# Block 1's norms on GpSimd, with the context rows loaded a job ahead

## The chip, the cores and the metric

The kernel runs on one core of a Trainium2 chip. A core has a matrix engine (PE, with its weight loads shown as PEld), VectorE (DVE), ScalarE (ACT), GpSimd (POOL) and SyncE (SP), which work side by side and wait for one another by semaphores. Data are in on-chip memory (SBUF), in the eight accumulator banks of PSUM, or in DRAM, from and to which DMA moves them. Each engine runs its own instructions in a fixed order, so an instruction that waits holds up all those behind it on its engine. A DMA is issued by one engine's queue and then runs by itself.

The metric is the device time of one execution, in microseconds, taken as the median of the runs; lower is better.

## The reference

The input is x, 16 batches × 256 rows × 512 channels in float32, a context of the same shape, and a padding mask. Two blocks run over x. The first (block 0) is a cross-attention block with a GELU MLP. The second (block 1) is the one that the change touches. Cut to its steps, with 16 heads of 32 channels:

```python
def layer(x, context):
    m0 = (any of x[b, s, :] != 0)          # rows in use, as 0 or 1
    x = layer_norm(x + mha(x, x, Wq1, Wk1, Wv1, m0, causal=True), ln1_g, ln1_b)
    m1 = (any of x[b, s, :] != 0)
    x = layer_norm(x + mha(x, context, Wq2, Wk2, Wv2, m1, causal=False), ln2_g, ln2_b)
    h = relu(x @ fc1_w.T + fc1_b) * m0
    x = layer_norm(x + (h @ fc2_w.T + fc2_b) * m0, ln3_g, ln3_b)
    return x

def _mha(x, kv, Wq, Wk, Wv, mask, causal):
    Q, K, V = x @ Wq, kv @ Wk, kv @ Wv     # per head, times the mask
    energy = Q @ K.T
    lengths = number of columns with energy[.., 0, :] != 0
    energy = -inf where column >= lengths (and where column > row, if causal)
    return (softmax(energy / sqrt(32)) @ V) * mask
```

Where the reference spells steps out with einsum, they stand here in words. The kernel masks the context's rows before the products with Wk2 and Wv2, which is the same as masking K and V. A layer norm subtracts the row's mean, multiplies by the inverse of its standard deviation, multiplies by a gain per channel and adds an offset per channel.

## The kernel before

Rows are handled in eight groups of two batches, which is 512 rows or four tiles of 128 rows × 512 channels. Block 1 has sixteen jobs: eight groups of self-attention (n = 0 to 7), then eight of cross-attention (n = 8 to 15). Its MLP over the eight groups comes behind them. A job has eight units (i, c), two batches by four sets of four heads, so 32 heads.

The main stream of job n − 1 (scores, softmax, values) is woven together with `feed(n)`, which makes what job n needs: q, k and v by matrix products, the transposes of its inputs, and the lengths of the rows in use. The order of PE's instructions is thereby written out by hand. The orders of DVE, ACT, POOL and SP come from a scheduler, which plays the program through on a timeline with its own estimates of durations and puts each instruction where it would be ready. Changing durations, buffers or engines of some instructions therefore moves others too.

What the change and the steps of the prediction touch:

- `ln_stats` (L244 to L248): the statistics of a tile (BN) and the variance plus epsilon on DVE, and the power −0.5 on POOL (L248). `layer_norm` adds two operations of DVE in which a row's mean or scale and a table of gains or offsets enter (L257, L258).
- `Mha.norm` (L1436 to L1443): when all channels of a batch's two tiles are through, their norms are queued in `att.later`. For a self job `nonzero` (L1369, DVE) then tests the finished rows, which gives the mask m1; the rows are stored to DRAM by SP (L1442). Later jobs load them again (`rows_of`, L1492) into one of three x tiles.
- `finish` (L1464 to L1473): z is scaled from PSUM to SBUF by DVE (L1466) and added to the x tile by POOL (L1473).
- `context_rows` (L1549 to L1552) loads one 128 × 512 tile of the context by SP; the tag `t512` with three places holds it, and also `junk` of the test and the MLP's `relu` and `y`. `context` (L1554 to L1562) multiplies it by m1 on POOL (L1559), transposes it on PE (L283, into `ps_t`), and asks for the tile three further on.
- `project_t` (L264) makes q and k; `split` (L131, L135, L136) takes them from PSUM as a high and a low half; `keep` (L384) stores them as `d` in DRAM, and `build` (L395, L399, L404) loads them again as `stack`, the shape that the scores need.
- `lengths` (L1397 to L1417) makes the row bias from the first token's energies: PE (`ps_e`, L1397), DVE (`lbias`, L1405 to L1413), and a small DMA to `dbias` (L1417). `first_token` (L1378, L1380, split at L139 and L140) prepares the first token's q.
- The scores (L414, `ps_s`, two PSUM banks), their row minimum in cross jobs (L425, L429, `mn`), the exponential on ACT (L439, `e`), the transposes of it (L455, `ps_pt`; taken out by DVE L459 or ACT L461, `pt`), and the reciprocal sums `rr` (L1451, L1452).
- The weights of the next kind of job are loaded in steps of the same queue, `att.later`, and split by POOL (L195, L198).
- `norm_table` (L1536 to L1546) loads a table of gains and offsets, broadcast to 128 partitions: ln1 in job 0, ln2 at the end of job 8's feed, and ln3 before the MLP. Two tables have places at a time (tag `lnt`).
- In the MLP, `up` makes relu (L1650) and its halves, and `down` makes `y` on ACT (L1656), adds it on POOL (L1657), and ends with a layer norm and the store to the output (L1661).

SP's DMAs use eight semaphores in a ring, so that a DMA is not issued before the one eight places earlier has landed.

Of the kernel before, what the change touches and what calls it, by code (L numbers as in the profile page):

```python
# [42 lines left out]
def kernel(ctx: ExitStack, tc: tile.TileContext, a, out):  # L43
# [1377 lines left out]
    def block1(mlp0):  # L1421
        tables, more = {}, {}

        class Mha(Job):
# [111 lines left out]
        def norm_table(name, n):  # L1536
            t = tables[name] = pool.tile([P, 2, C], F32, tag="lnt", name=name)
            rows = a[name].rearrange("o (r c) -> o r c", c=C)
            nc.sync.dma_start(
                out=t.rearrange("p r c -> p (r c)"),  # L1540
                in_=bcast(rows[:, :2].rearrange("o r c -> o (r c)"), 2 * C),
            )
            if n == 3:
# [5 lines left out]
        def context_rows(n, t):  # L1549
            if n < len(jobs) and jobs[n].cross and (n, t) not in cxs and t < G:  # L1550
                cx = cxs[n, t] = pool.tile([P, C], F32, tag="t512", name="cx", bufs=3)
                nc.sync.dma_start(out=cx, in_=of("ctx", jobs[n].g)[:, t, :])  # L1552

        def context(n, t):  # L1554
            job = jobs[n]
            if t == 0:
                job.c_t = inputs("c_t")
            cx = cxs[n, t]
            nc.gpsimd.tensor_scalar(cx, cx, job.m[:, t : t + 1], None, ALU.mult)  # L1559
# [23 lines left out]
        def feed(n):  # L1583
# [5 lines left out]
            for c in range(KC):  # L1589
# [34 lines left out]
            for t in range(3 if n + 1 > NG else 2):  # L1624
# [4 lines left out]
            if n == NG:  # L1629
                norm_table("ln2", 2)  # L1630
# [14 lines left out]
        def up(g, c):  # L1645
# [3 lines left out]
            r = pool.tile([P, N], F32, tag="t512", name="relu", bufs=3)  # L1649
# [3 lines left out]
        def down(g, t):  # L1653
            x = xs[g][:, t, :]
            y = pool.tile([P, C], F32, tag="t512", name="y", bufs=3)
# [4 lines left out]
            layer_norm(pool, x, tables["ln3"][:, 0, :], tables["ln3"][:, 1, :])  # L1660
# [84 lines left out]
```

## Time and profile before

| | |
|---|---|
| runs | 2740.61, 2741.23, 2743.34 us |
| median | 2741.23 us |
| profiled execution | 2734.54 us |
| its span, first to last instruction | 2732.8 us |
| mean granted PE clock | 0.993 |
| PE busy | 2655.3 us, 97% |
| DVE busy | 2053.2 us, 75% |
| ACT busy | 1816.8 us, 66% |
| POOL busy | 604.5 us, 22% |
| block 1 in the trace | from about 1370 us to the end |
| a steady self job | 66.3 us |
| a steady cross job | 74.7 us |

The profiled execution is one run; what lies in it between the span and its time is 1.74 us. Busy time of an engine counts its instructions' durations. A line of waits names the engine and line that waited, the engine and line that it waited for, the total, the count and the longest. A line of a group names the line, the engine, the operation, its output and inputs with shape and type, the count, the busy time, and the mean of one in nanoseconds, then the idle time before it and what ended that. A stretch of the span is told as its bounds, its length, the busy time of PE, PEld, DVE, ACT and POOL with counts, PE's granted clock, the share of DMA time and its rate.

### The profile page before, as it was taken

To read this page: it belongs to the slowest core of one execution; us is meant where nothing else is said; L and a number is where in the kernel's file an instruction comes from. 1 tells how busy PE (TensorE), PEld (TensorE's weight loads), DVE (VectorE), ACT (ScalarE), POOL (GpSimd) and SP (SyncE) were. 2 spreads that over 40 slices of the span, in tenths; PEclk is the share of its full clock that TensorE was granted. 3 is DMA by queue.
4 is the path that set the end of the run, shared out by engine and by line. 5 is a ranking of instruction groups with operands and counts; after the bars stand their busy time and mean duration, and the time that the engine had idled before them with its cause. 6 is when DMAs were issued, how large, how long until landed. Compare 5 with 4: busy or idle time off the path is not lost.

```text
span 2732.8 us, 56709 instructions
## 1 busy us (share of the span) xinstructions
PE 2655.3 (97%) x19030; PEld 2245.1 (82%) x19030; DVE 2053.2 (75%) x5963; ACT 1816.8 (66%) x5278; POOL 604.5 (22%) x676
## 2 busy tenths in 40 slices
PE   8999999999899999999989999999999999999998
PEld 6777777777899999999978877887777777777787
DVE  7776667757846569999957777777778777777887
ACT  4877777778555555444547888877777777777522
POOL 2222212114301101111221111115212222113334
PEclk9999999999999999999999999999999999999999
DMA  6666556556323344443475656667666665565321
GB/s 231 189 194 182 171 173 190 186 166 174 112 112 136 124 163 171 166 169 140 155 232 174 192 192 195 196 199 213 183 198 191 190 194 183 183 189 161 104 90 51
DMA packets 287808, 465.40 MB, mean 170 GB/s; under 512 B 36256, under 2 KB 188320, under 8 KB 279328
## 3 DMA queue, kind: packets, MB, share of 16 engines
q1 hardware_dynamic: 287520, 461.78, 52.5%
q8 instruction: 153, 2.51, 0.4%
q14 instruction: 135, 1.11, 0.1%
HBM read 284.97 MB, written 176.69 MB: 169 GB/s over the span
## 4 chain that ended last, share of the span: by engine, by line
PE 80%; DVE 11%; DMA 3%; issue 3%; ACT 2%; POOL 1%; SPq 0%; POOLq 0%; DVEq 0%; ACTq 0%
PE ps_p L264 20%; PE ps_v L264 15%; PE down L1142 10%; PE ps_pt L455 9%; PE ps_s L414 6%; PE ps_z L474 6%; PE up_sc L1026 5%; PE up_pt L1026 3%; PE up_mm L1026 3%; PE ps_t L283 2%; ACT e L439 1%; DVE st L244 1%; DVE e L429 1%; DVE c_t L145 1%; PE ps_z L1464 1%
## 5 line engine op out<-in xcount | busy, mean ns | idle before, releaser
L439 ACT ACTIVATE e<-e,mn 128x256 f32<-128x256 f32 (+1 forms) x1024 | 487.5, 481 | 58.5 <-DVE mn L429 56.4
L461 ACT COPY pt<-ps_pt 128x512 f32<-128x512 f32 (+1 forms) x696 | 378.6, 547 | 175.8 <-PE ps_pt L455 163.8
L455 PE MATMUL ps_pt<-ident,e 128*128 128x128 f32 x2816 | 435.5, 273 | 14.5 <-DVE lbias L1406 7.9
L455 PEld LDWEIGHTS ps_pt<-ident,e 128*128 128x128 f32 x2816 | 336.1, 140 | 53.9 <-ACT pt L461 6.5
L414 PE MATMUL ps_s<-stack 97*128 97x256 f32 (+1 forms) x1536 | 331.6, 297 | 12.4 <-ACT e L439 5.6
L414 PEld LDWEIGHTS ps_s<-stack 97*128 97x128 f32 (+1 forms) x1536 | 268.6, 190 | 72.8 <-ACT e L439 13.2
L439 ACT ACTIVATE e<-ps_s,mn 128x256 f32<-128x256 f32 x512 | 241.4, 484 | 53.2 <-DVE mn L425 42.9
L1142 PE MATMUL down<-w_h,c_t 128*128 128x256 f32 x900 | 255.5, 285 | 5.4 <-DVE c_t L145 5.4
L1473 POOL TENSOR_TENSOR x<-x,zz 128x256 f32<-128x256 f32 x128 | 95.8, 748 | 724.6 <-DVE zz L1466 671.0
L1142 PE MATMUL down<-w_h,x_t 128*128 128x256 f32 x868 | 245.8, 283 | 0.7 <-ACT x_t L144 0.7
L1142 PE MATMUL down<-w_l,x_t 128*128 128x256 f32 x868 | 246.2, 284 | 0.0
L429 DVE CUSTOM_DVE_ANT_0 e<-mb,ps_s 128x256 f32<-128x256 bf16 x512 | 192.7, 415 | 70.6 <-PE ps_s L414 68.7
L248 POOL TENSOR_TENSOR rstd<-rstd,nhalf 128x1 f32<-128x1 f32 x192 | 141.0, 740 | 385.0 <-DVE rstd L247 384.3
L264 PE MATMUL ps_p<-x_t,q_h 128*128 128x512 f32 x640 | 215.3, 417 | 4.2 <-DVE qk L131 2.1
L425 DVE TENSOR_REDUCE mn<-ps_s 128x2 f32<-128x512 f32 x256 | 175.3, 685 | 49.2 <-PE ps_s L414 47.0
L429 DVE CUSTOM_DVE_ANT_0 e<-tri,ps_s 128x128 f32<-128x128 f32 (+1 forms) x512 | 160.2, 346 | 54.9 <-PE ps_s L414 52.9
L474 PE MATMUL ps_z<-pt,v 128*32 128x256 f32 (+1 forms) x3072 | 198.2, 368 | 2.0 <-DVE pt L459 1.9
L439 ACT ACTIVATION_READ_ACCUMULATOR e<-e,mn 128x1 f32 x1024 | 197.6, 193 | 0.0
L1142 PEld LDWEIGHTS down<-w_h,c_t 128*128 128x128 f32 x900 | 171.3, 191 | 7.3 <-DVE c_t L145 7.3
L1142 PEld LDWEIGHTS down<-w_h,x_t 128*128 128x128 f32 x868 | 166.5, 192 | 1.1 <-ACT x_t L144 0.9
L1142 PEld LDWEIGHTS down<-w_l,x_t 128*128 128x128 f32 x868 | 165.2, 190 | 0.0
L474 PEld LDWEIGHTS ps_z<-pt,v 128*32 128x32 f32 x3072 | 82.3, 109 | 98.4 <-issue 28.5
(256 smaller groups left out, 7232.0 us busy)
## 6 DMA issues: line engine op xcount, KB each, us to landing
stack<-d SPq DMA_DIRECT2D x1152, 128.0 KB
d<-qk SPq DMA_DIRECT2D x192, 512.0 KB
hid<-ho SPq DMA_DIRECT2D x32, 1024.0 KB
raw<-hid SPq DMA_DIRECT2D x32, 1024.0 KB
x<-xd SPq DMA_DIRECT2D x128, 256.0 KB
xd<-x SPq DMA_DIRECT2D x96, 256.0 KB
xin<-in_x_dram SPq DMA_DIRECT2D x32, 256.0 KB
xr<-in_x_dram SPq DMA_DIRECT2D x32, 256.0 KB
```

Source lines behind the costliest of these rows:

```text
L248: nc.gpsimd.tensor_tensor(out=rstd[:, 1:2], in0=rstd[:, 0:1], in1=nhalf, op=ALU.pow)
L264: nc.tensor.matmul(ps, w[p], x[q], start=(k == 0 and i == 0), stop=(k == kc - 1 and i == 2))
L414: nc.tensor.matmul(ps[:, t, :], u.st[: self.rows, 0, j, ts(t, P)], u.st[: self.rows, 1, j, :], start=True, stop=True,)
L425: nc.vector.tensor_reduce(mn, ps, AX.X, ALU.min)
L429: nc.vector.tensor_tensor_reduce(out=e[:, at], in0=bias[t], in1=ps[:, t, : job.width[t]], scale=-SC, scalar=BIG, op0=ALU.add, op1=ALU.min, ...
L439: nc.scalar.activation(e[:, at], ps[:, t, :] if bias is None else e[:, at], AF.Exp, bias=mn[:, t : t + 1], scale=-1.0, accum_out=u.rs[:, t ...
L455: nc.tensor.transpose(pp[:, ts(x, P)], e[:, at : at + P], ident)
L461: nc.scalar.copy(pt[:, :n], pp[:, :n])
L474: nc.tensor.matmul(z[ts(j, D), w[0] * P :], job.v[u.i * NT + mc][:, u.c * P + j * D : u.c * P + (j + 1) * D], u.pt[j][:, x0 * P : (x0 + le ...
L1026: nc.tensor.matmul(ps[:, mm, :], w[p][:, k, :], x[q][:, k, :], start=(first and mm == k == j == 0), stop=(k == 1 and j == 2), skip_group_c ...
L1142: nc.tensor.matmul(ps[:, t, :], x[p][:, mm, ts(t, P)], w[r][:, bo, :], start=(q == mm == t == j == 0), stop=(q == self.NS - 1 and mm == 1 ...
L1473: nc.gpsimd.tensor_tensor(out=xv, in0=xv, in1=zz, op=ALU.add)
```

## The change

The sixty norms of block 1's attention jobs other than the last cross group's four leave DVE for POOL after the statistics: one operation with mean and scale, one multiplication by the gain table, one addition of the offset table. The stores of these rows go by POOL's queue. The test of a self job's rows writes bfloat16 into a place of its own.

Context rows have four places of their own (tag `cx`). All four tiles of a job are asked for in the feed of the job before, `context` asks for none, and DVE masks them. The tables of norms share one place; ln2 is asked for in job 9's feed, behind the second q product, and ln3 is loaded as two tiles into context places. The MLP's `relu` and `y` take places of the tags `e` (five) and `pts` (six).

```diff
+    def layer_norm_pool(pool, x, gain, offset):
+        mean, rstd = ln_stats(pool, x)
+        nc.gpsimd.tensor_scalar(x, x, mean, rstd, ALU.subtract, ALU.mult)
+        nc.gpsimd.tensor_tensor(out=x, in0=x, in1=gain, op=ALU.mult)
+        nc.gpsimd.tensor_tensor(out=x, in0=x, in1=offset, op=ALU.add)
...
             def norm(self, t):
                 x, table = self.x[:, t, :], tables["ln2" if self.cross else "ln1"]
-                layer_norm(pool, x, table[:, 0, :], table[:, 1, :])
+                last = self.cross and self.g == NG - 1
+                norm = layer_norm if last else layer_norm_pool
+                norm(pool, x, table[:, 0, :], table[:, 1, :])
                 if not self.cross:
-                    junk = pool.tile([P, C], F32, tag="t512", name="junk", bufs=3)
+                    junk = pool.tile([P, C], BF16, tag="junk", name="junk", bufs=1)
                     nonzero(junk, x, m1[:, self.g, t : t + 1])
-                nc.sync.dma_start(
+                (nc.sync if last else nc.gpsimd).dma_start(
                     out=xd[3 if self.cross else 2][self.g][ts(t, P), :], in_=x
                 )
...
         def norm_table(name, n):
-            t = tables[name] = pool.tile([P, 2, C], F32, tag="lnt", name=name)
             rows = a[name].rearrange("o (r c) -> o r c", c=C)
...
-            if n == 3:
+            if n == 2:
+                t = tables[name] = pool.tile([P, 2, C], F32, tag="lnt", name=name, bufs=1)
...
+            else:
+                tables[name] = [pool.tile([P, C], F32, tag="cx", name=name, bufs=4) for r in range(2)]
+                for r, t in enumerate(tables[name]):
+                    nc.sync.dma_start(out=t, in_=bcast(rows[:, r], C))
...
-                cx = cxs[n, t] = pool.tile([P, C], F32, tag="t512", name="cx", bufs=3)
+                cx = cxs[n, t] = pool.tile([P, C], F32, tag="cx", name="cx", bufs=4)
...
-            nc.gpsimd.tensor_scalar(cx, cx, job.m[:, t : t + 1], None, ALU.mult)
-            cost = transposed(job.c_t, cx, t)
-            context_rows(n, t + 3)
-            return cost
+            nc.vector.tensor_scalar(cx, cx, job.m[:, t : t + 1], None, ALU.mult)
+            return transposed(job.c_t, cx, t)
...
+                if n == NG + 1 and c == 1:
+                    norm_table("ln2", 2)
                 if job.cross:
                     for t in FRONTS[c]:
-                        context_rows(n, t)
                         yield context(n, t)
...
-            for t in range(3 if n + 1 > NG else 2):
+            for t in range(G):
                 context_rows(n + 1, t)
...
-            if n == NG:
-                norm_table("ln2", 2)
...
-            r = pool.tile([P, N], F32, tag="t512", name="relu", bufs=3)
+            r = pool.tile([P, N], F32, tag="e", name="relu", bufs=5)
...
-            y = pool.tile([P, C], F32, tag="t512", name="y", bufs=3)
+            y = pool.tile([P, C], F32, tag="pts", name="y", bufs=6)
...
-            layer_norm(pool, x, tables["ln3"][:, 0, :], tables["ln3"][:, 1, :])
+            layer_norm(pool, x, *tables["ln3"])
```

By the scheduler's order PE's instructions stand as before. DVE has 120 operations fewer (60 each of L257 and L258) and 32 more (the masks). POOL has 32 operations fewer, 180 more, and 60 DMA issues. SP has 60 stores fewer. The loads of job 8's four context tiles, and their masks, are moved by it to job 0's time at the beginning of block 1, since their places are free from the start.

More of the change, by code (lines that the diff above doesn't have):

```diff
@@ L1536, in norm_table @@
         def norm_table(name, n):
-            t = tables[name] = pool.tile([P, 2, C], F32, tag="lnt", name=name)
             rows = a[name].rearrange("o (r c) -> o r c", c=C)
[L1539 to L1542, printed above, removed]
-            if n == 3:
+            if n == 2:
+                t = tables[name] = pool.tile([P, 2, C], F32, tag="lnt", name=name, bufs=1)
+                nc.sync.dma_start(
+                    out=t.rearrange("p r c -> p (r c)"),
+                    in_=bcast(rows[:, :2].rearrange("o r c -> o (r c)"), 2 * C),
+                )
+            else:
+                tables[name] = [pool.tile([P, C], F32, tag="cx", name=name, bufs=4) for r in range(2)]
+                for r, t in enumerate(tables[name]):
+                    nc.sync.dma_start(out=t, in_=bcast(rows[:, r], C))
                 t = tables["fc2_b"] = pool.tile([P, C], F32, name="fc2_b", bufs=1)
```

## Prediction

> **What bounds the kernel now.** I read the totals by engine, the chain that ended last, the stretches of block 1, then PE's waits there, then the groups of instructions that the change touches.
>
> ```profile
> span 2732.8 us, 56709 instructions
> PE 2655.3 (97%) x19030; PEld 2245.1 (82%) x19030; DVE 2053.2 (75%) x5963; ACT 1816.8 (66%) x5278; POOL 604.5 (22%) x676
> PE 80%; DVE 11%; DMA 3%; issue 3%; ACT 2%; POOL 1%; SPq 0%; POOLq 0%; DVEq 0%; ACTq 0%
> ```
>
> PE is busy for 97% of the span. No edit here takes a matmul away, so whatever is gained must come out of PE's idle time (and out of the clock lost behind it), and whatever is lost is new PE idle time. The stretches give it by stage (us, then PE, PEld, DVE, ACT, POOL busy with counts, then PE clock, DMA share, GB/s): all of block 1, a steady self job, the last self job with the change to cross jobs, the first cross job, a steady cross job, the MLP end, and two pieces of the change.
>
> ```profile
> 1370.00:2732.80 1362.80, 1317.88 (x9008) 1053.63 (x9008) 1036.90 (x3339) 938.71 (x3025) 326.76 (x345) 0.99 0.56 176
> ...
> 1562.60:1628.90 66.30, 65.42 (x482) 52.91 (x481) 50.62 (x237) 53.22 (x185) 9.59 (x12) 1.00 0.60 192
> 1827.80:1896.30 68.50, 64.70 (x460) 51.47 (x459) 49.93 (x226) 49.61 (x172) 28.53 (x30) 0.95 0.75 228
> 1896.30:1971.00 74.70, 69.70 (x499) 56.12 (x498) 55.72 (x227) 55.09 (x188) 23.00 (x24) 0.98 0.65 199
> 2120.30:2195.00 74.70, 73.31 (x531) 58.12 (x530) 58.50 (x145) 55.64 (x180) 14.91 (x16) 1.00 0.59 185
> 2570.00:2732.80 162.80, 154.15 (x706) 123.82 (x704) 130.25 (x249) 44.43 (x71) 64.11 (x57) 0.98 0.23 81
> ...
> 1876.00:1884.00 8.00, 4.83 (x33) 3.15 (x31) 4.47 (x19) 3.16 (x13) 6.85 (x8) 0.74 0.96 229
> 1908.00:1916.00 8.00, 5.64 (x35) 4.57 (x37) 6.42 (x26) 4.73 (x17) 5.34 (x5) 0.84 0.63 214
> ```
>
> A steady self job leaves 0.9 us of PE idle in 66.3, a cross job 1.4 in 74.7; DVE and POOL have room in both. What PE waited for in block 1 (total, times, longest):
>
> ```profile
> PE ps_pt L455 <- DVE lbias L1406: 7.9, 7, 3.2
> PE ps_e L1397 <- ACT qk L135: 5.2, 1, 5.2
> PE ps_s L414 <- DVE rr L1452: 3.0, 5, 0.6
> PE ps_t L283 <- POOL cx L1559: 3.0, 2, 2.4
> PE ps_p L264 <- DVE qk L131: 2.1, 1, 2.1
> ```
>
> Five of the seven lbias waits are about 0.87 us each, one in a steady cross job; the 3.2, the 2.4 and the 2.1 are the change to cross jobs (1877 to 1915 us). The five rr waits are 0.6 each, one per self job. All the PE gaps that I could list behind 1370 us add up to 36.5 us: the ceiling of any gain before clock.
>
> **The change part by part.** These are the groups that it moves (us busy, mean ns):
>
> ```profile
> L257 DVE SCALAR_TENSOR_TENSOR x<-x,mv,ln 128x512 f32<-128x512 f32 x96 | 77.1, 805 | 0.0
> L258 DVE SCALAR_TENSOR_TENSOR x<-x,rstd,ln 128x512 f32<-128x512 f32 x96 | 70.5, 741 | 6.7 <-POOL rstd L248 6.1
> L1559 POOL TENSOR_SCALAR cx<-cx,m 128x512 f32<-128x512 f32 x32 | 51.6, 1613 | 68.9 <-DMA cx<-in_ctx_dram 65.9 <-PE ps_p L264 1.3 <-DVE mn L429 1.0
> L1657 POOL TENSOR_TENSOR x<-x,y 128x512 f32<-128x512 f32 x32 | 44.1, 1407 | 46.5 <-ACT y L1656 46.5
> ```
>
> *Norms.* 60 of the 64 norms of block 1's jobs move (the last cross group and the MLP's 32 stay). DVE loses 60 × (0.805 + 0.741) = 92.8 us. POOL gains 60 × (1.61 + 2 × 1.41) = 266 us, priced by its mask row and its y-add row; for three operations of 2-input kind it would be 254, and with the subtract-and-multiply at the slowest mask seen (1.96) 287. Per job of four tiles DVE drops by 6.2 us, POOL rises by 17.7: a self job from 9.6 to 27 of 66, a cross job to 26 of 75 after its masks leave. POOL stays under 45%.
>
> *Masks.* 32 operations leave POOL (−51.6 us) and join DVE. DVE has no such row: 0.42 (the 128x512 cast, L139) from below, 0.68 (L1369) from above; I take 0.48, nearer the cast, so +15 us. DVE net: −6.2 a self job, −4.3 a cross job.
>
> *What this is worth on PE's path.* The 0.6 us (self) and 0.87 us (cross) gaps come just behind DVE's burst of statistics and norms, where DVE comes late to rr or lbias. Taking 3.1 us of norm operations out of each burst of two tiles should close most. Five self gaps × 0.6 gives 3.0 and five cross gaps × 0.87 gives 4.4, both taken whole. Bounds: 0 and 7.4.
>
> *The change to cross jobs.* The 2.36 us wait on a masked cx row goes, since job 8's four tiles are now loaded and masked at the beginning of block 1. The 2.11 on qk (DVE in its burst) I halve. The 3.17 on lbias has DVE itself waiting 1.42 us for a small DMA, and the ACT ahead of it 2.30 for DVE; I halve it too. Sum 2.4 + 1.05 + 1.6 = 5.0, bounds 2.4 and 7.6. Behind these gaps the granted clock fell to 0.74 and 0.84. With the 0.83 and 0.95 of the neighbouring 8 us, (1 − clock) × busy adds up to 3.8 us; I take half, 1.9.
>
> The Trainium skill, "TensorE: Matmul & The Clock Gate", Part 1, says that PE's clock halves after an idle window of about 3.4 us and comes back after as long a busy one. The 0.74 stands behind a gap of only 3.17 us here; by that rule no gap left would cost clock, all 3.8 us would come back, and the sum would be 1.9 us lower.
>
> *New wait: DVE on a context row.* In a steady cross job a mask no longer waits on POOL but in DVE's order, two running minima (L425) behind the last q split (L131). SP issues the store of that split first and the next job's rows straight behind (0.34 + 0.38 us by SP's rows). Rows land 3.80 us after issue (row at 2054.75) up to 5.93 (1984.20). A head takes 74.7/32 = 2.33 us, so DVE is there some 2.5 to 3.5 us after the split and waits 1 to 4 us (0.72 + 3.80 − 3.5 to 0.72 + 5.93 − 2.5) for a mask that nobody needs for a job. Behind it stand L425, L459 and the rr of the running heads. PE has two score banks, so about 1.9 us pass free; cost 0 to 2.2 us a job, I take 0.6 × 7 = +4.2 (a wait of 2.5, the middle; bounds 0 and +15), because three of the four masks stand further behind their load.
>
> *New wait: DVE on POOL.* The nonzero test (L1369) of a self job reads the finished norm. By the order it stands seven heads (14.5 us or more) behind the statistics; POOL's row of work for two tiles, two pow at 0.89, the residual add L1473 at 0.75 and 2 × 4.4, ends 11.3 us after them if POOL is not held. Slack 3 us: cost 0, bound +1 us × 8. The cover is gone if POOL's operations here run a quarter slower.
>
> *POOL's queue.* 60 stores go to POOL, 60 of SP's 64 leave L1442. No row has a store issued by POOL: by SP's rows 0.3 to 0.43 each; bound 0 to one mask (1.6). On POOL that is at most 6.4 us a job, in free time. Each job's x loads (L1492) wait until the stores of two jobs before have landed, now 8 us later; in the steady jobs 7 to 9 us remain before PE's transposes. SP is in order, and stack builds behind it (L395, L399, L404) have some 13 us. Cost 0, bound +1 us × 13.
>
> The Trainium skill, "SBUF — State Buffer", "SBUF: two separate sides", speaks against this: GpSimd and a DVE instruction with two SBUF inputs take one port pair exclusively, and descriptors for a GpSimd-issued DMA are starved meanwhile; it advises issuing from SP or ACT. No such store is in this trace. By the page's example (620 ns grown to 3100) each store would be 2.5 us later, a third of the slack above, so the sum would stay.
>
> *Sharing.* DVE operations that overlap POOL are longer here: the small tok cast (L139) 0.17 us alone, 0.49 on average beside POOL. Added over 1430 to 2570 us this is 5.8 us. POOL's 327 us becomes about 540, so DVE's excess grows by 3.8 us over 15 jobs; I put +0.5 on PE's path.
>
> *Start of block 1.* Job 8's 4 × 256 KB replace the ln3 load there, 512 KB ahead of the k store instead of 768 KB, 768 KB more behind. The 5.2 us wait on ACT qk (behind d<-qk, landing 7.75 us) may shrink by 1; later stores come later. Taken +1, bounds ±3.
>
> *MLP end.* relu and y change rings (five and six places), ln3 sits in two cx places. The same operations on the same engines; 0, bounds ±1.
>
> Sum: −3.0 − 4.4 − 5.0 − 1.9 + 4.2 + 0.5 + 1.0 = −8.6. The profiled execution took 2734.5 us, so 2725.9 in its terms. It lies 6.7 us below the median of the runs (2741.2), which gives 2732.6. A difference of 0.2% (5.5 us) is about what a measurement of this kernel can tell.
>
> **Rivals.**
>
> *A. DVE stands at a mask or a test, slower.* Place: the first mask of each steady cross job. If the row lands 7 us behind its issue (a d<-qk store took 7.75 at 1400), DVE waits some 4.5 us, PE loses 2.6 × 7 = 18, and gaps of that length pull the clock as at 1877 (1.2 us each), 8 more. The other terms of the sum give −12.8, so +13, about 2754. It decides from a wait of 3.7 us: 1.8 over PE's free 1.9, × 7 = 12.8. For it: POOL waited for cx rows 23 times, up to 5.8 us. Against: most waits there were 2 to 3 us, and the 512 KB store ahead is on the same queues in before too.
>
> *B. Hidden anyway.* PE is 97% busy, and each burst's gap can be taken over by the next late thing: ACT's e (5.6 us in 13 waits) or the mean dbias DMA. Then only the cx wait's 2.4 and some clock return, less 1 to 3 of new waits: 2738 to 2742, say 2740.
>
> *C. POOL late, slower.* If its two-pointer subtract takes over 2.5 us or ports hold it, a pair of tiles takes 15 us or more, the test blocks DVE, and the x loads block SP ahead of stack builds. 1 to 2 us × 15 jobs plus clock: 2755 to 2765. The trace's POOL rows leave 3 us, so it is least likely.
>
> **How the numbers follow.** Forecast 0.50, B 0.22, A 0.18, C 0.10. The forecast's own range is 2724 (all gaps and clock back, masks free: −17) to 2737. Over all cases 2724 to 2754 holds about 8 in 10; C lies mostly above. Faster: forecast 0.47 of its 0.50, B 0.04: 0.51. Within 0.2%: 0.03 + 0.16 = 0.19. Slower: B 0.02, A 0.18, C 0.10: 0.30.
>
> **What would show it.** Right: steady self jobs of 65.7 and cross jobs of 74 to 74.4 us; no lbias wait of 0.87 behind the bursts; no "ps_t <- cx" near 1912 and a clock over 0.95 from 1876 to 1916; POOL 26 to 28 us a job; DVE's wait at the mask under 2 us. Wrong: DVE idle ended by "DMA cx" or by POOL's x over 3 us a job with PE's ps_s or ps_pt behind it (A, C), POOL's subtract over 2.5 us (C), or job lengths unchanged (B).

## The result, and the profile after

The changed kernel takes 2751.07 us (median of 7 runs, 2746.20 to 2754.09) against 2741.57 for the kernel before, timed beside it (median of 7, 2739.90 to 2744.33). The ratio is 1.003, with a 95% interval of 1.002 to 1.0039: it is 0.3% slower, where 0.3% faster was forecast. Two later measurements, on two different chips, gave 1.0061 (1.0049 to 1.0074) and 1.0014 (1.0004 to 1.0023). The sign is the same each time; the size is not.

The totals and the chain of the profiled execution (2750.62 us):

```profile
span 2748.9 us, 56602 instructions
PE 2668.2 (97%) x19030; PEld 2249.7 (82%) x19030; DVE 2052.9 (75%) x5875; ACT 1812.7 (66%) x5278; POOL 840.2 (31%) x884
PE 78%; DVE 10%; DMA 5%; ACT 4%; issue 2%; POOL 1%; SPq 0%; POOLq 0%; ACTq 0%; DVEq 0%
```

VectorE was to lose some 78 us. It lost 0.3 in the whole span, because many of the operations left to it became longer, as told below. GpSimd rose to 564 us in block 1, where about 540 was forecast. The stretches that answer to those of before (block 1, a steady self job, a steady cross job, the two pieces around the stop near 2480 us, and the MLP's end):

```profile
1370.00:2748.90 1378.90, 1331.36 (x9042) 1060.49 (x9040) 1040.65 (x3259) 936.75 (x3028) 564.01 (x553) 0.99 0.56 174
1569.00:1634.60 65.60, 65.16 (x484) 52.87 (x481) 50.42 (x229) 52.59 (x184) 28.65 (x28) 1.00 0.62 194
2120.30:2193.75 73.45, 73.23 (x532) 58.05 (x536) 56.31 (x140) 55.59 (x181) 28.79 (x28) 1.00 0.61 188
...
2476.00:2484.00 8.00, 3.46 (x30) 2.53 (x27) 6.31 (x8) 4.33 (x14) 7.70 (x9) 0.97 0.48 140
2484.00:2492.00 8.00, 7.42 (x34) 5.31 (x35) 1.90 (x3) 3.25 (x9) 0.38 (x1) 0.61 0.09 33
...
2580.00:2748.90 168.90, 154.07 (x684) 119.97 (x684) 136.13 (x245) 40.45 (x63) 56.08 (x52) 0.98 0.22 78
```

The steady jobs did become shorter: 65.6 us against 66.3, 73.45 against 74.7. So the gain is there, and is given back elsewhere. PE's idle time in block 1 is 37.7 us against 36.5, so the old gaps were replaced by new ones. Those 1.2 us are little beside what block 1 lost. PE's clock took more: (1 − clock) × busy, counted as in the prediction, is 12.3 us in block 1 against 6.2 before. The longest waits (total, times, longest):

```profile
PE ps_pt L462 <- ACT pt L468: 9.8, 12, 2.9
PE ps_e L1404 <- ACT qk L135: 3.4, 1, 3.4
PE ps_t L290 <- DMA x<-xd: 3.0, 1, 3.0
PE ps_s L421 <- DVE mn L436: 2.9, 2, 2.4
PE ps_z L481 <- DVE pt L466: 2.7, 2, 2.2
```

Of the old list the 0.87 us waits on lbias, the 0.6 us waits on rr and the wait on a masked cx row are gone.

Where the time went can be followed instruction by instruction, because PE's order is the same in all the kernels here. The table gives the start of ACT's instructions in a profile less the start of the same instruction in the profile of before (us, the median over a stretch of up to one job that begins at the time in the first column). A falling number is time gained, a rising one time lost. The columns are the changed kernel, its two later profiles (`after_again` and `after_same`), and two kernels told below: the kernel before with the MLP's places alone (`before_rings`), and the best one found (`both_sp`).

| before's time | changed | later 1 | later 2 | places alone | best |
|---|---|---|---|---|---|
| 1000 (block 0) | 5.6 | 3.4 | 3.2 | 0.0 | 5.6 |
| 1452 | 6.5 | 4.9 | 6.0 | 2.0 | 7.4 |
| 1848 (end of self jobs) | 3.0 | 5.3 | 2.7 | 1.9 | 4.7 |
| 2046 | 0.5 | 4.1 | -2.3 | 0.7 | 1.7 |
| 2442 (end of steady cross jobs) | -6.4 | -2.4 | -9.1 | 1.1 | -5.0 |
| 2485 | 0.8 | 6.9 | -7.6 | 1.1 | -4.2 |
| 2520 | 5.0 | 11.0 | -3.5 | 0.4 | -5.4 |
| 2550 | 4.9 | 10.9 | -3.6 | 0.2 | -5.5 |
| 2694 | 14.8 | 20.7 | 6.1 | 10.1 | -1.0 |

Block 0 is untouched by the change, and differs from profile to profile by up to 6 us; what its 5.6 us is stays open. From 1330 us on (5.2 there) the changed kernel loses 1.3 us at the start of block 1, gains 3.4 in the self jobs to 1848, 2.5 over the change of jobs to 2046 and 7.0 in the cross jobs to 2442, then loses 7.3 near 2480, 4.2 near 2520, and 9.8 in the MLP. That is 9.6 us net, close to the 9.5 between the medians.

### The profile page after: what moved, and what is told of

It is laid out like the page before. It is cut to its first block, busy times and chain, and to the rows that moved or that the text cites. A ratio compares the mean times of both kernels' runs of the same rounds, so it can differ in the third digit from the quotient of the medians.

```text
span 2748.9 us, 56602 instructions
## 1 busy us (share of the span) xinstructions
PE 2668.2 (97%) x19030; PEld 2249.7 (82%) x19030; DVE 2052.9 (75%) x5875; ACT 1812.7 (66%) x5278; POOL 840.2 (31%) x884
## 4 chain that ended last, share of the span: by engine, by line
PE 78%; DVE 10%; DMA 5%; ACT 4%; issue 2%; POOL 1%; SPq 0%; POOLq 0%; ACTq 0%; DVEq 0%
PE ps_p L271 19%; PE ps_v L271 14%; PE down L1149 10%; PE ps_pt L462 9%; PE ps_z L481 6%; PE ps_s L421 6%; PE up_sc L1033 5%; PE up_pt L1033 3%; PE up_mm L1033 3%; PE ps_t L290 2%; ACT e L446 1%; DMA d<-qk 1%; DVE e L436 1%; PE ps_z L1473 1%; PE ps_e L1404 1%
## 5 line engine op out<-in xcount | busy, mean ns | idle before, releaser
L468 ACT COPY pt<-ps_pt 128x512 f32<-128x512 f32 (+1 forms) x696 | 376.8, 545 | 148.2 <-PE ps_pt L462 132.3
L462 PE MATMUL ps_pt<-ident,e 128*128 128x128 f32 x2816 | 436.4, 273 | 13.7 <-ACT pt L468 11.3
L248 POOL TENSOR_TENSOR rstd<-rstd,nhalf 128x1 f32<-128x1 f32 x192 | 122.1, 640 | 421.6 <-DVE rstd L247 375.5
L436 DVE CUSTOM_DVE_ANT_0 e<-mb,ps_s 128x256 f32<-128x256 bf16 x512 | 192.3, 413 | 70.6 <-PE ps_s L421 69.6
L481 PE MATMUL ps_z<-pt,v 128*32 128x256 f32 (+1 forms) x3072 | 207.1, 370 | 10.0 <-DVE pt L466 5.6
L432 DVE TENSOR_REDUCE mn<-ps_s 128x2 f32<-128x512 f32 x256 | 175.0, 684 | 53.4 <-PE ps_s L421 50.7
L436 DVE CUSTOM_DVE_ANT_0 e<-tri,ps_s 128x128 f32<-128x128 f32 (+1 forms) x512 | 159.0, 345 | 52.9 <-PE ps_s L421 51.1
```

The costliest lines, as they stand in the source:

```text
L248: nc.gpsimd.tensor_tensor(out=rstd[:, 1:2], in0=rstd[:, 0:1], in1=nhalf, op=ALU.pow)
L432: nc.vector.tensor_reduce(mn, ps, AX.X, ALU.min)
L436: nc.vector.tensor_tensor_reduce(out=e[:, at], in0=bias[t], in1=ps[:, t, : job.width[t]], scale=-SC, scalar=BIG, op0=ALU.add, op1=ALU.min, ...
L462: nc.tensor.transpose(pp[:, ts(x, P)], e[:, at : at + P], ident)
L468: nc.scalar.copy(pt[:, :n], pp[:, :n])
L481: nc.tensor.matmul(z[ts(j, D), w[0] * P :], job.v[u.i * NT + mc][:, u.c * P + j * D : u.c * P + (j + 1) * D], u.pt[j][:, x0 * P : (x0 + le ...
```

## The experiments

The theory after the result had three parts. First, the MLP is slow because of the places of relu and y. Second, two-operand work on GpSimd holds up VectorE's small operations on SBUF. Third, rows stored late by GpSimd stop PE near 2520. The main rival was that of the prediction, VectorE waiting at the context masks.

### The MLP's places

y in the tag `e`, the places that the change gives to relu, on the changed kernel (`y_ring`):

```diff
-            y = pool.tile([P, C], F32, tag="pts", name="y", bufs=6)
+            y = pool.tile([P, C], F32, tag="e", name="y", bufs=5)
```

> The changed kernel with the MLP's y in the places of relu (tag e, five) instead of places of its own (pts, six). The four additions of y on GpSimd then stand together ahead of each MLP group's norms again, as before the change; nothing else moves but a few instructions of the last cross job. Theory (port): the additions that the own places let run a group ahead fall into VectorE's norm burst and block it; the MLP loses 1.5 us a group by that. Expected: MLP groups back from 25.9 to 24.4 us each, about 9 us less than the changed kernel, so 2741 to 2743, level with before. Rival (the context masks' waits on DVE or the GpSimd stores cost the time): the MLP's groups have neither, so the groups stay at 25.9 and the time at 2750.

The places alone, on the kernel before (`before_rings`):

```diff
-            r = pool.tile([P, N], F32, tag="t512", name="relu", bufs=3)
+            r = pool.tile([P, N], F32, tag="e", name="relu", bufs=5)
...
-            y = pool.tile([P, C], F32, tag="t512", name="y", bufs=3)
+            y = pool.tile([P, C], F32, tag="pts", name="y", bufs=6)
```

> The kernel before, with only the MLP's relu and y moved to the places that the change gives them (e, five; pts, six). Theory (port): the additions run a group ahead here too, and the MLP's groups go from 24.4 to 25.9 us: 9 to 10 us slower, about 2751, as slow as the whole change. Rival (the MLP is slow because of what the attention's change leaves behind, such as late stores or the ln3 table): no change, 2741.

Measured: the places alone make the kernel before slower, 2743.63 against 2737.27, ratio 1.0029 (1.0018 to 1.0040). That is 6.4 us, where 9 to 10 was expected. In the profile the loss lies in the MLP: the table's column runs from 0.2 at 2550 to 10.1 at 2694, 1.5 us a group, just as in all three profiles of the changed kernel. PE, which waited for nothing in the MLP before, now waits for VectorE there, above all in these two rows:

```profile
PE ps_p L264 <- DVE x_t L136: 2.3, 5, 0.5
PE ps_v L264 <- DVE c_t L140: 2.1, 5, 0.4
```

Two timelines of GpSimd over one group show what the places do. The kernel before, then the kernel with the places alone (start, duration, operation, idle before):

```profile
2617.45 5.42 POOL L1657 TENSOR_TENSOR x<-x,y 128x512 f32<-128x512 f32 x4 [7.92 <-ACT y L1656]
```

```profile
2624.37 1.30 POOL L1657 TENSOR_TENSOR x<-x,y 128x512 f32<-128x512 f32 x1 [2.61 <-issue]
2626.33 0.92 POOL L248 TENSOR_TENSOR rstd<-rstd,nhalf 128x1 f32<-128x1 f32 x1 [0.66 <-DVE rstd L247]
2627.61 1.30 POOL L1657 TENSOR_TENSOR x<-x,y 128x512 f32<-128x512 f32 x1 [0.36 <-issue]
2631.07 0.92 POOL L248 TENSOR_TENSOR rstd<-rstd,nhalf 128x1 f32<-128x1 f32 x1 [2.16 <-DVE rstd L247]
2631.97 1.29 POOL L1657 TENSOR_TENSOR x<-x,y 128x512 f32<-128x512 f32 x1
```

Before, y shares three places with relu, so the next group's y has to wait for relu, and the four additions run together ahead of VectorE's norms. With six places of its own y runs ahead, and the additions fall one by one between the norms. There VectorE's operations on two tiles in SBUF and its cast meet them (kernel before, then places alone, some 105 us of the MLP each; mean of one in ns behind the comma):

```profile
L258 DVE SCALAR_TENSOR_TENSOR x<-x,rstd,ln 128x512 f32<-128x512 f32 x16 | 11.9, 746 | 1.9 <-POOL rstd L248 1.4
L139 DVE CAST c_t<-relu 128x512 fp32r<-128x512 f32 x18 | 7.7, 426 | 15.5 <-ACT relu L1650 15.5
```

```profile
L258 DVE SCALAR_TENSOR_TENSOR x<-x,rstd,ln 128x512 f32<-128x512 f32 x17 | 20.2, 1189 | 2.3 <-POOL rstd L248 1.8
L139 DVE CAST c_t<-relu 128x512 fp32r<-128x512 f32 x18 | 12.3, 686 | 14.5 <-ACT relu L1650 14.1
```

One operation a group was also slow before (L257, 1021 ns on average there, 742 here), so the net is 0.44 + 0.26 - 0.28 us, by four: 1.7 us of VectorE a group. In `y_ring` the loss falls from 1.5 to 0.6 us a group, and the same in `both` below, where VectorE still takes the product's result ahead of the transposed rows and PE waits for it (L1670, 2.3 us in five). Its time hardly followed: 2744.96 (2733.48 to 2758.08), ratio 1.0029 (1.0014 to 1.0043), where a time level with before was expected (2737.27 on that chip). Its profile has new stops in the attention in place of what the MLP gave back, which led to the next point.

### The last two cross groups

The norms and stores of the last two cross groups left to VectorE and SyncE (`last_two`), and both edits together (`both`):

```diff
-                last = self.cross and self.g == NG - 1
+                last = self.cross and self.g >= NG - 2
```

> The changed kernel, with the norms and stores of the last two cross groups (not only the last) left to VectorE and SyncE. Theory (port and late store): the 8.6 us lost at 2478 us come from a 128x8 product of VectorE that stood 3.0 us behind GpSimd's pile of norm and weight operations, and the 4 to 5 us at 2520 from rows whose GpSimd store came late. With these norms off GpSimd both go: 12 to 13 us less, 2738 to 2740. Rival (weights alone crowd GpSimd there, which the kernel before has too): the stop at 2478 stays, and the time at 2747 to 2750.

> The two edits together: y in relu's places, and the last two cross groups' norms on VectorE. If the two losses are separate, 21 to 22 us less than the changed kernel: 2728 to 2731, 10 to 13 us below before. If they are the same lost time (one hidden behind the other), 2738 to 2741.

Measured: `last_two` 2738.73, ratio 1.0011 (1.0001 to 1.0022). From 2442 to 2550 us its profile loses 2.2 us, where the changed kernel's lost 11.3: the stop near 2520 is gone and of that near 2480 some 3 us are left. `both` 2737.09 (2729.60 to 2743.10), ratio 1.000 (0.9989 to 1.0010). So the two together come out below each alone, though the intervals of `both` and `last_two` overlap. The scatter is much wider than that of before (13.5 us against 7.5), and the 10 us gain expected did not come. The profile of `both` shows where its missing time is. It has two gaps of 1.8 us in the self jobs (at 1512.98 and 1582.27), each worth some 3.5 us with the clock behind it. VectorE at the first of them, then GpSimd:

```profile
1508.17 0.42 DVE L1475 TENSOR_TENSOR zz<-ps_z,rr 128x256 f32<-128x256 f32 x1
1508.52 5.62 DVE L1387 TENSOR_TENSOR own<-hmask,tok 128x16 f32<-128x16 f32 x1
1514.06 0.28 DVE L436 CUSTOM_DVE_ANT_0 e<-tri,ps_s 128x128 f32<-128x128 f32 x1
```

```profile
1508.41 1.30 POOL L259 TENSOR_TENSOR x<-x,ln 128x512 f32<-128x512 f32 x1
1509.68 0.72 POOL L1482 TENSOR_TENSOR x<-x,zz 128x256 f32<-128x256 f32 x1
1510.37 1.26 POOL L259 TENSOR_TENSOR x<-x,ln 128x512 f32<-128x512 f32 x1
1511.60 2.50 POOL L260 TENSOR_TENSOR x<-x,ln 128x512 f32<-128x512 f32 x2
```

A product of 128 x 16 elements, 0.17 us long when alone, lasts 5.62 us: from just behind the start of GpSimd's run of five two-operand operations to its end. The exponentials' minima (L436) stand behind it, then ACT, then PE. The stop near 2480 us has the same shape, a product of rr (L1461, 128 x 8) of 3.02 us that ends with the second of two weight operations on GpSimd:

```profile
2480.66 0.20 DVE L1460 RECIPROCAL rr<-rs 128x8 f32<-128x8 f32 x1 [0.35 <-ACT e L446]
2480.89 3.02 DVE L1461 TENSOR_TENSOR rr<-rr,m 128x8 f32<-128x8 f32 x1
2483.84 0.68 DVE L466 COPY pt<-ps_pt 128x512 f32<-128x512 f32 x1
```

```profile
2480.72 0.64 POOL L1451 DMA_DIRECT2D xd<-x  x1
2481.39 2.50 POOL L198 TENSOR_TENSOR k_l<-wst,k_h 128x512 fp32r<-128x512 f32 x2
```

That hold is only part of the stop. A gap of 2.9 to 3.0 us just ahead of it, in which PE waits for ACT's copies (L468), is there in all profiles with the norms of the last but one cross group on GpSimd. In the later profile where the hold is missing (later 2), 1.5 us are lost over 2442 to 2485 instead of 7.3. But `sp_stores` and `sp_same`, told below, have no hold either and lose 6.7 and 4.7 us there, with another PE wait of 1.7 to 2.3 us for ACT's exponentials ahead of the gap. So the hold's own share of the 7.3 us is not settled. ACT's order at the gap has the copy behind two casts of transposed rows and four exponentials; that this order sets the gap is a reading, not tried. With the last two groups' norms on VectorE the wait for the copies is gone, and PE waits 1.1 to 2.0 us for lbias instead (`last_two`, `both`, and `both_sp` below).

### Taking the operands away

Two products without a second operand from SBUF, on `both` (`no_pair`; the names in angle brackets stand for broadcasts that the kernel writes out):

```diff
-            at = pool.tile([P, NB], F32, tag="tok", name="tok")
-            nc.vector.tensor_copy(at, q[:, 0 : N : S])
+            at = q[:, 0 : N : S]
...
-                nc.vector.tensor_tensor(rr, rr, <self.m>, ALU.mult)
...
-                nc.vector.tensor_tensor(zz, pz, <u.rr>, ALU.mult)
+                for t in range(NT):
+                    nc.vector.scalar_tensor_tensor(
+                        zz[:, t], pz[:, t], <self.m of t>, <u.rr[:, t]>, ALU.mult, ALU.mult)
```

> The kernel with both edits (y in relu's places, the last two cross groups' norms on VectorE), and two small products of VectorE in the attention no longer with two operands from SBUF: the first token's own reads its token from PSUM instead of a copy, and the mask of rr is multiplied into the scaling of z (two scalar-tensor-tensor operations on PSUM by unit in place of one product, and no separate product on rr). Theory (port): these two products are what stands for whole runs of GpSimd work (5.6 us once, 3.0 us once); with them gone no VectorE operation of the attention takes over 2 us, the stops of 1.8 us in the self jobs and the one at 1890 us go, and the time falls 5 to 8 us under the kernel with both edits: ratio to before 0.997 to 0.998. Rival (those stops are late instruction issue or DMA): they stay, and the ratio stays at 1.000.

One-operand operations on GpSimd, on the changed kernel (`ts_only`). They multiply by 1 and add 0, so the kernel leaves out the gain and the offset of these norms:

```diff
-        nc.gpsimd.tensor_tensor(out=x, in0=x, in1=gain, op=ALU.mult)
-        nc.gpsimd.tensor_tensor(out=x, in0=x, in1=offset, op=ALU.add)
+        nc.gpsimd.tensor_scalar(x, x, 1.0, None, ALU.mult)
+        nc.gpsimd.tensor_scalar(x, x, 0.0, None, ALU.add)
```

> The changed kernel with GpSimd's two two-operand operations of each norm (times gain, plus offset) replaced by one-operand operations on the same tile (times 1, plus 0), so the gain and the offset of the norms ln1 and ln2 are left out in all but the last cross group. As many GpSimd operations on as many bytes, in time as long or longer. Theory (GpSimd's tensor-tensor operations hold VectorE, its tensor-scalar operations don't): VectorE's excess in the attention falls from 52 to 60 us to 15 or less, the stop at 2485 us (8.6 us with its clock) and the random ones in the self jobs go; the late rows near 2520 and the MLP's 9 to 10 us stay. 8 to 12 us below the changed kernel, ratio to before 1.000 to 1.003. Rival (any GpSimd work on SBUF holds VectorE, or GpSimd's lateness itself costs): excess and stops stay, ratio 1.005 or more.

`no_pair` was a miss: 2739.12, ratio 1.0012 (0.9999 to 1.0025), where 0.997 to 0.998 was expected. The two products are held no longer, but the holds went to what stood next: the comparison of lbias (L1419 there, one operand from SBUF) took 4.06 us twice and 3.92 once, against 0.40 alone. So a single operand from SBUF is enough on VectorE's side.

`ts_only` shows GpSimd's side. Its three norm operations take 2.08, 1.51 and 1.50 us, 5.1 together against 4.7, so GpSimd is busier than in the changed kernel. The groups of rr, lbias and masks in the attention (1430 to 2570 us), the changed kernel first, then `ts_only`:

```profile
L1461 DVE TENSOR_TENSOR rr<-rr,m 128x8 f32<-128x8 f32 x128 | 40.9, 319 | 2.9
L1420 DVE TENSOR_SCALAR lbias<-cols,n 8x256 f32<-8x256 f32 x60 | 36.0, 600 | 1.2
L1573 DVE TENSOR_SCALAR cx<-cx,m 128x512 f32<-128x512 f32 x32 | 26.0, 812 | 14.4 <-DMA cx<-in_ctx_dram 14.4
```

```profile
L1420 DVE TENSOR_SCALAR lbias<-cols,n 8x256 f32<-8x256 f32 x60 | 32.0, 534 | 1.1
L1461 DVE TENSOR_TENSOR rr<-rr,m 128x8 f32<-128x8 f32 x128 | 24.3, 190 | 2.8
L1573 DVE TENSOR_SCALAR cx<-cx,m 128x512 f32<-128x512 f32 x32 | 19.7, 617 | 17.3 <-DMA cx<-in_ctx_dram 17.2
```

VectorE's excess is what its operations take over their median length with GpSimd idle. Added up from 1430 to 2570 us over these three kinds and the first token's product and its two splits (L1387, L139, L140), it is 9 us in the kernel before, 58 in the changed one and 28 here, where 15 or less was expected. No such operation is over 1.5 us, and the self jobs have no stop. The loss from 2442 to 2485 is 2.6 us instead of 7.3. The time is 2749.45, ratio 1.0033 (1.0021 to 1.0045), over the 1.000 to 1.003 expected and within the changed kernel's own three (1.0014 to 1.0061): the norms being longer, the rows are later still, and PE's wait for them near 2520 grew from 3.0 to 7.0 us.

Sorted by what GpSimd ran when such an operation of VectorE began, the changed kernel's mean excess is 0.08 us behind the subtract-and-multiply (L258, one tile, 47 times), 0.69 behind the gain (L259, two tiles, 40 times) and 0.75 behind the offset (L260, 14 times). In `ts_only` it is 0.21 behind the first and 0.11 behind the second one-tile operation that stand there instead. Reads of PSUM, the statistics, the reciprocals and the operations that accumulate show no excess.

### The two halves

Two kernels part the change. `ctx_only` is the change without any norm on GpSimd, by the line below. `norm_only` is the kernel before with only the norms and their stores moved, as in the change.

```diff
-                last = self.cross and self.g == NG - 1
+                last = True
```

> The changed kernel with all norms on VectorE and all stores on SyncE: the context rows, their masks on VectorE, the tables and the MLP's places alone. Theory (port): no gain in the self jobs (66.3 us each), cross jobs 74.7 or a little more for 1.8 us of masks on VectorE, no stop near 2478 or 2520, the MLP's groups at 25.9 us: 7 to 10 us slower than before. Rival (the masks' wait for DMA is what costs): cross jobs 75.5 us and more, and 13 to 16 us slower.

> The kernel before with only the norms of all but the last cross group on GpSimd, and their stores on its queue; masks on GpSimd, places and tables as before. Theory: self jobs 0.6 to 0.7 us and cross jobs about 1 us shorter, the stop near 2478 and the late rows near 2520 there (some 13 us), the MLP's groups at 24.4 us: between 4 us faster and 4 us slower than before. Rival (the gains come from the context rows): jobs as long as before and 10 us or more slower.

Both are worse than the whole, which took 2752.41 on the same chip: 2757.51, ratio 1.008 (1.0067 to 1.0093), and 2761.90, ratio 1.0097 (1.0082 to 1.0111). In `ctx_only` the self jobs are as long as before and the cross jobs about 3 us longer (by the table's count 3.6 to 20.2 us from 2046 to 2442, over 5.3 jobs), with VectorE's waits for context rows of 17.9 us in nine over that stretch, up to 3.9. This is the rival's number and more: 20.5 us slower than before, where the theory had 7 to 10. In the changed kernel the same waits are 8.5 us in eight, up to 1.8, and the cross jobs are shorter than before. The two rows, `ctx_only` first:

```profile
DVE cx L1573 <- DMA cx<-in_ctx_dram: 17.9, 9, 3.9
```

```profile
DVE cx L1573 <- DMA cx<-in_ctx_dram: 8.5, 8, 1.8
```

That the masks' waits are what lengthens the cross jobs of `ctx_only` is read from these rows, not tried by itself, and why they are longer there stays open.

`norm_only` has the self jobs' gain (0.7 us a job, but for one hold of 5.61 us at 1507) and the cross jobs' (over 1 us), no loss in the MLP, and two large stops that the theory did not have. Its longest PE waits:

```profile
PE ps_t L290 <- POOL cx L1568: 25.3, 2, 15.2
```

The masks, still on GpSimd, stand in order behind the norms there. To take the masks off GpSimd as well is not enough (`norm_mask`: `norm_only` with the edits of `last_two` and `no_pair` and the line below, but the context rows' three shared places as before).

```diff
-            nc.gpsimd.tensor_scalar(cx, cx, job.m[:, t : t + 1], None, ALU.mult)
+            nc.vector.tensor_scalar(cx, cx, job.m[:, t : t + 1], None, ALU.mult)
```

> The kernel before with the norms of all but the last two cross groups on GpSimd and stored by its queue, the masks on VectorE, and the first token's own and the mask of rr without two SBUF operands; the places, tables and loads of the context rows and the MLP's places as before. Theory: the self jobs' 0.6 to 0.7 us and the cross jobs' 1 to 1.5 us are won, the MLP's groups stay at 24.4 us, no mask stands behind norms on GpSimd (the kernel with norms alone stopped 15 and 10 us there), and the stop near 2485 is gone: 5 to 12 us faster than before, ratio 0.996 to 0.998. Rival (the masks' wait for late context rows costs in the cross jobs what the norms win): ratio 0.999 to 1.002.

It takes 2764.83, ratio 1.0091 (1.0078 to 1.0104), outside both forecasts, with the same two stops:

```profile
PE ps_t L290 <- DVE cx L1562: 23.1, 2, 13.4
```

There the rows share places with the test's junk tile, and the test now ends only behind GpSimd's norms. By that reading, which no run isolates, the places of their own are what the norms on GpSimd need. Its cross jobs do not gain either: 3.6 us are lost from 2046 to 2442, with VectorE's waits for context rows of 20.5 us in fourteen from 2046 to 2465. That the two halves of the change are not independent is shown: each alone is slower than both.

### The store's queue

The stores by SyncE, on the changed kernel (`sp_stores`):

```diff
-                (nc.sync if last else nc.gpsimd).dma_start(
+                nc.sync.dma_start(
```

> The changed kernel with the rows' stores issued by SyncE instead of GpSimd. Theory (the stores' issue on GpSimd is a small part: 0.6 us each, 2.4 us a job): the stops behind GpSimd stay, SyncE stands in order behind the finished norms and stack builds come later; within 4 us of the changed kernel, ratio 1.002 to 1.007. Rival (GpSimd's queue is what makes the rows late): the stop near 2520 goes and the time falls by 4 us or more.

It took 2739.84, ratio 0.9998 (0.9988 to 1.0007), better than the theory had it. But the rival's sign did not come, for the stop near 2520 is still there, and so is the gap near 2480:

```profile
PE ps_pt L462 <- ACT pt L468: 9.5, 12, 2.9
PE ps_t L290 <- DMA x<-xd: 2.1, 1, 2.1
```

PE's wait for the rows near 2520 is 2.1 us here and 2.4 in `sp_same`, against 2.9 to 3.0 in the three profiles of the changed kernel. So most of it is not the queue: the norms on GpSimd end late, whoever issues the store. With these norms on VectorE (`last_two`) the wait is gone.

The changed kernel had not been timed on the same chip, so it was run again on one chip with this one and with two that add the other edits: `both` with this line (`both_sp`), and `no_pair` with it (`no_pair_sp`).

> The changed kernel once more. If the stops behind GpSimd come and go by when VectorE's small products meet GpSimd's runs, its times spread wider than those of before (10 us and more from lowest to highest), about a median of 1.003 of before, and the profile has its stops at other places than the first one; if the loss is fixed in the order of instructions, the same stops at the same places.

> The changed kernel, on the same chip as the three that follow. Ratio to before 1.003 to 1.006, as in its two measurements so far.

> The changed kernel with the rows' stores issued by SyncE, beside the changed kernel on one chip. If issue by GpSimd costs time (its 0.6 us lengthen GpSimd's runs, and the rows land later), it is 6 us or more below the changed kernel here too, ratio to before 0.998 to 1.001. If the earlier difference was the chip's, both lie within 3 us.

> y in relu's places, the last two cross groups' norms on VectorE, and all stores by SyncE. If the three losses add up: 5.8 us (MLP) and 9 to 13 us (2485 and 2520 us) below the changed kernel with SyncE's stores, ratio to before 0.994 to 0.996. If the store's loss is the same as that of 2520 us, 0.997 to 0.999.

> The same, and the first token's own and the mask of rr without two SBUF operands. If VectorE held behind GpSimd costs on PE's path beside that, 2 to 5 us below the kernel before this one: ratio 0.993 to 0.995. If the holds only move to the operations left (the lbias comparison, the first token's casts, as without SyncE's stores), the same ratio within 0.001.

| kernel | median, us | runs | ratio to before |
|---|---|---|---|
| after_again (another chip) | 2752.41 | 2750.30 to 2756.53 | 1.0061 (1.0049 to 1.0074) |
| after_same | 2745.37 | 2737.18 to 2749.30 | 1.0014 (1.0004 to 1.0023) |
| sp_same | 2740.96 | 2737.86 to 2743.34 | 1.0001 (0.9992 to 1.0009) |
| both_sp | 2730.58 | 2728.16 to 2733.65 | 0.9962 (0.9949 to 0.9975) |
| no_pair_sp | 2735.11 | 2726.80 to 2736.87 | 0.9972 (0.9961 to 0.9983) |

The store's queue is worth 4.4 us between the medians on that chip (0.13% by the ratios, whose intervals just touch), between the two forecasts of 6 and more and of 3 and less. `after_same` itself came out below the 1.003 to 1.006 expected. The scatter is 5.5 us from lowest to highest against 12.1 there, but was 14.1 in the first measurement of `sp_stores`, so it is not all the queue's. The profiles show one difference. In nine profiles of kernels with two-operand norms and stores on GpSimd, VectorE's small operations were held over 1.8 us thirty times, in eight of the nine (up to seven in one; the ninth is that of after_same). In the four with stores by SyncE, and in `ts_only`, `ctx_only`, `before_rings` and the kernel before, never. `after_again`, as expected of stops that come and go, had four, three of them where the first profile had none (at 1508, 1877 and 2026 us). Why the holds reach over several operations only where GpSimd also issues stores was not settled. The sum of the excess does not tell the two apart: it is 51 us in `sp_same`, near the changed kernel's 58.

`both_sp` adds the three repairs, and beats both kernels: 0.38% faster than before, about 10 us, just short of the 0.994 to 0.996 expected if the losses add up. Left in it are the MLP's groups, still 0.6 us too long, and the stops at the change to cross jobs. `no_pair_sp` doesn't improve on it.

## Why the prediction was wrong

Three terms of the sum failed, all priced at 0 to 0.5 us: "MLP end" (measured 9.8, shown by `before_rings`), "Sharing" (measured as the stop near 2480, 7.3 with a PE wait that has another cause in it) and "POOL's queue" (measured 4.2). The time lies near rival A's 2754, but not for A's reason, so that is luck. Term by term:

- **Norms.** Priced at 1.61 + 2 x 1.41 = 4.4 us a tile on GpSimd; measured 2.08 + 1.30 + 1.31 = 4.7, and the store's issue 0.60 within its bounds. Right in sum.
- **Gaps behind the bursts.** Forecast -3.0 in the self jobs and -4.4 + 4.2 in the cross jobs. Measured 0.7 us a self job (-3.4 to 1848 us) and 1.25 us a cross job (-7.0 from 2046 to 2442 us). Right in kind, and more in the cross jobs than the 4.4 taken whole; the +4.2 for masks that wait was an overestimate, since those waits stayed at 1.8 us and less, under the 1.9 us that PE has free. Rival A, which it fed, did not come, except in `ctx_only`.
- **Sharing.** It was scaled by GpSimd's busy time (5.8 us to 9.6, +0.5 on PE's path); measured 58 us, by the count above that gives 9 for before. PE lost little by that sum: `sp_same` has 51 us of it and gains 14 us from 1330 to 2442, where the changed kernel gains 11.6. What PE lost came where a hold on a short operation lasted, as at 2481, and in the MLP. The error was in the measure: the busy time of before is mostly one-operand masks, 128x1 powers and half-size additions, which hold VectorE little, and the change added 120 full-size operations with two operands in runs of four and five. The trace of before had the hint, sorted as above: a mean excess of 0.36 us behind a weight's two-operand operation (L198), in six meetings, against 0.10 behind a mask (L1559), in 29.
- **Skill, weighed in the prediction.** The Trainium skill, "SBUF — State Buffer", "SBUF: two separate sides", was right against this change in its main point, that GpSimd and a VectorE instruction with two SBUF inputs shut each other out for a whole instruction, and its advice to issue from SP was worth 4.4 us here. Its reason for that advice, descriptors that are kept waiting, it gives for VectorE's two-port modes, and no run shows it: GpSimd's stores landed 3.3 us after their issue, and no landing of SyncE's is on record to set beside that. The trace differs in two places: a GpSimd operation with one tile from SBUF cost VectorE 0.08 us on average and not its whole length, and a hold could reach over five instructions in a row (5.62 us), not one.
- **Change to cross jobs.** Forecast -6.9. Little of it came: from 1782 to 1985 us the profile gains only about 2, no more than the steady jobs gain. The 2.36 us wait on a cx row went, but stops of 2.7 us at 1883 and 2.4 at 1918 took the place, on ACT's and VectorE's order in the same burst. The clock was to give back 1.9; over block 1 it took 6.1 more, behind the new gaps.
- **POOL's queue.** "Cost 0, bound +1 us x 13" held in the jobs and failed at one place that was not looked at: the MLP's second group, whose rows are loaded into the x tile of job 14. Its load waits for the stores of rows whose norms end late on GpSimd, and PE waited 3.0 us for it; 4.2 us with the clock. The issue by GpSimd is the smaller part, since SyncE's stores leave 2.1 to 2.4 us of that wait.
- **MLP end.** "0, bounds +-1" was wrong by 9.8 us, the largest single loss. The step took the same operations on the same engines for the same time, and did not ask when six places let y be made. With them the additions on GpSimd fall between VectorE's norms, whose scale-and-offset operations (L258) go from 746 to 1189 ns in `before_rings`. It is the sharing again, brought about by the order: what else changes when a tile gets more places is the order.
- **Start of block 1.** Forecast +1, measured 1.3 from 1330 us to the stretch from 1452. The size is right, but not the reason: the wait on ACT's qk fell from 5.2 us to 3.4, and a new wait of 1.5 us for ACT's copies came at 1478.

The losses add up to 1.3 + 7.3 + 4.2 + 9.8 = 22.6 us, the gains to 3.4 + 2.5 + 7.0 = 12.9, near the 3.0 + 4.4 + 5.0 + 1.9 = 14.3 of the forecast. So the gains were about right as a sum, by luck, since the change of jobs gave 4.4 less than forecast and the cross jobs 2.6 more. Three losses that were costed at 0 to 0.5 us turned the sign. Rival C (GpSimd late) named the mechanism, but at the test and with a subtract of over 2.5 us, neither of which came.

## What to carry to other kernels

When work moves from VectorE to GpSimd, price it on both: sort the VectorE operations that touch SBUF by what GpSimd runs when they start, and count the new operations by their operands, not by busy time. Then ask which of them stand on the critical chain, for one held operation of 0.2 us there can cost more than the sum of the others. And a tile that gets more places may be made earlier, so its consumers move in time even where no instruction is added; look at what they will now stand beside.

## What was not expected of the hardware

- GpSimd's 128x512 operations with two tiles held VectorE's operations on SBUF by 0.69 and 0.75 us on average, those with one tile by 0.08 (a row's mean and scale) to 0.21 (a constant); operations of VectorE that read PSUM were untouched by both (the running minima, L432, took 0.66 to 0.70 us in the kernel before and in the changed one alike).
- A hold can last over a run of GpSimd operations: 5.62 us for a 0.17 us product, seen in five profiles at that same line, and only where the stores too were issued by GpSimd with norms of two operands.
